# Indirect transfers of a macaron transformer layer, entered by the experts' products instead of at three fixed places of a unit

## The chip, the cores and the metric

The kernel runs on one core of one Trainium2 chip. The metric is device microseconds (us) of one execution. Before the change, three runs took 700.78, 701.87 and 702.69 us; their median is 701.87 us. A separate execution was profiled. TensorE is called PE in the views (its weight loads PEld), VectorE DVE, ScalarE ACT, GpSimd POOL and SyncE SP.

## What is computed

The input x has 8 sequences of 512 tokens with 128 features, in float32. A layer is half a feed-forward step, attention, and another half feed-forward step, each on the layer-normalised x:

```python
x = x + 0.5 * _L0_ffn_ref(_layernorm(x, axis=-1), router_w, router_b, W1, b1, W2, b2)
x = x + _L0_attn_ref(_layernorm(x, axis=-1), w_qkv, w_o, log_xi)
x = x + 0.5 * _L0_ffn_ref(_layernorm(x, axis=-1), router_w, router_b, W1, b1, W2, b2)
```

The feed-forward step is a mixture of 8 experts (128 to 512 to 128 features, ReLU between); a router picks two of them for each token, with a softmax over the two scores as their weights:

```python
logits = jnp.einsum('bsd,de->bse', x, router_w) + router_b
topk_scores, topk_idx = jax.lax.top_k(logits, TOP_K)      # TOP_K = 2
topk_gates = jax.nn.softmax(topk_scores, axis=-1)
...
    h = jax.nn.relu(jnp.einsum('bsd,df->bsf', h_in, w1) + bb1)
    y = jnp.einsum('bsf,fd->bsd', h, w2) + bb2
    return (acc + y * c[..., None], None)                  # c: this expert's weight per token
```

Attention is causal, with 16 heads of 8 features; some heads have a rotary embedding, some a linear decay in the distance.

## The kernel before

**Groups.** Sequences go through the experts in groups: f0 (sequences 0 and 1), f1 (2, 3, 4), f2 (5, 6, 7) for the first feed-forward step, g0, g1, g2 with the same sequences for the last. A group reserves a fixed number of rows for each expert: 351 in f0 and g0, 480 in the others. Four things happen to a group:

- *Routing* (`route`, one call for each sequence) normalises x, takes the router's products, and computes for every token the row of its two experts. The normalisation's reciprocal root, `rstd`, is a `pow` on POOL (recorded at L474, which is the line of the helper `InTurn` through which all such POOL work goes); DVE's four `xn` operations (L769) need it, PE's transposes `xnT_ps` (L784) need those, DVE copies the result (`xnT`, L786), and PE's router products `lg_ps` (L814) follow.
- Eight *scatters* for each sequence (L875) write its tokens to the experts' rows in HBM (`xs`). Each is one indirect DMA that POOL issues, for 128 tokens and one of their two experts.
- The *experts* (`experts`): SP fetches an expert's rows (`xb`, L933); PE transposes them (a `turn`, `xbT_ps`, L976); four *wide* products (`z`, L989) give the hidden features, evicted with ReLU by ACT or DVE (L996, L998); three or four *down* products (`y`, L1013) follow, evicted by DVE (`ysb`, L1017). Turns, wide and down products are the group's *pieces*, which come one at a time from a generator.
- The results come back. For f0, f1, f2 and g0, SP writes an expert's rows to `ys` (L1024), and eight *gathers* for each sequence (`yt`, indirect, L474 through the helper) fetch each token's two rows; DVE adds them to x (L1073). For g1 and g2 every eviction is *sent* to its token's place by an indirect DMA (`ys`, L957), four for each expert, and SP collects whole sequences later (`collect`: `yr`, L1110; DVE adds, L1114; output, L1120).

**Units.** The program is a list of units, numbered -30 to 125, which `surround` (L1427) writes out one after the other. Units 0 to 95 are the *core*: each holds one step of attention (scores, exponentials on ACT, causal mask on DVE, values) with pieces of a group between. Units -30 to -1 (the *prologue*) and 96 to 125 (the *tail*) have no attention; the prologue runs f0's pieces and then f1's, the tail the rest of g1's and all of g2's. `plan` says which group's pieces are run in which units, and each unit takes an equal quota. A table `due` says in which unit the steps of routing, projection, collection and so on come.

**Order.** PE, ACT, DVE and SP run their instructions in the order in which the program was written. POOL's order is fixed by dependencies in `in_turn` (L621): everything that POOL does through the helper comes after all transfers that were entered earlier, and the reverse; only scatters and sends of one run among themselves have no order.

**Transfers.** The indirect transfers wait in two queues of the program's author, not of the chip: `jobs` (scatters and gathers) and `results` (sends). Each call of `transfer` (L650) writes out the next one; with `second=True` it does so only if some job is urgent, or if more than four jobs are queued and no result. `behind_mark` (L635) makes each transfer wait for the eviction of the last wide or down product that was written before it (or for a causal mask in the core); this eviction is its *mark*. In `surround`, `transfer` is called at three fixed places of a unit: after the first piece (L1458), at the end (L1478, `second=True`), and in units from 96 on also at half of the quota when more than two transfers are queued (L1472 to L1475).

Of the kernel before, what the change touches and what calls it, by code (L numbers as in the profile page):

```python
# [21 lines left out]
B, N, D = 8, 512, 128  # L22
# [4 lines left out]
E, FF = 8, 512  # L27
C = FF // P
# [19 lines left out]

ROOMS = [(2, 351, False), (3, 480, False), (3, 480, False), (3, 480, True), (3, 480, True)]
CAP = max(cap for _, cap, _ in ROOMS)  # L50
NOWHERE = 1e6
CT = -(-CAP // P)
STOP = object()
# [395 lines left out]
class Group:  # L449


    def __init__(self, seqs, cap, key, xs, ys, tagged):
        self.seqs, self.cap, self.key, self.xs, self.ys = seqs, cap, key, xs, ys
        self.tagged, self.width = tagged, D + 2 * tagged
        self.ct = -(-cap // P)
        self.rows = cap // self.ct
        assert self.ct * self.rows == cap
        self.parts = [(t, min(3 if cap > 4 * P else 4, self.ct - t))
                      for t in range(0, self.ct, 3 if cap > 4 * P else 4)]
        self.placed = 0  # L460
        self.pieces = E * (len(self.parts) * (1 + C) + self.ct) + 1


# [19 lines left out]
class Main:  # L483
    def __init__(self, tc, ctx, aps):
# [15 lines left out]


        self.jobs, self.results, self.mark = deque(), deque(), None
        self.adds, self.unit = deque(), 0
        const = self.const

# [31 lines left out]
        for e in range(4):  # L537
# [28 lines left out]
            out=before, in_=before, compare_op=ALU.is_gt, fill=0.0, base=0,  # L566
# [8 lines left out]
            out=self.earlier, in_=self.earlier, compare_op=ALU.is_gt, fill=0.0, base=0,  # L575
# [6 lines left out]
            out=self.keep, in_=self.keep, compare_op=ALU.is_ge, fill=0.0, base=0,  # L582
# [67 lines left out]
    def transfer(self, second=False):  # L650

        if self.jobs and (
            not second or any(urgent for urgent, _ in self.jobs)
            or (len(self.jobs) > 4 and not self.results)
        ):
            self.jobs.popleft()[1]()
        elif self.results:
            self.results.popleft()()

    def additions(self):  # L660

# [262 lines left out]
    def experts(self, g):  # L924
# [3 lines left out]
        rows = g.rows  # L928
# [27 lines left out]
        def send(e, t, ys):  # L956
            ins = nc.gpsimd.indirect_dma_start(  # L957
                out=g.ys[:, :],
                out_offset=bass.IndirectOffsetOnAxis(ap=home[e][:rows, t : t + 1], axis=0),
                in_=ys[:rows, t, :], in_offset=None,  # L960
            ).ins
            tc.declare_no_dep(ins, group=f"ys_{key}", reason="no two rows have the same home")
            tc.add_to_no_dep_group(f"ys_{key}", ins)
            self.in_turn(ins, scatter=True)
            self.behind_mark(ins)

        def up(e, xb):

            xT = self.fp.tile([P, CAP], FP, tag="xT", name=f"xT_{key}_{e}")
            h = self.fp.tile([P, C, CAP], FP, tag="h", name=f"h_{key}_{e}")  # L970

            def turn(t0, nt):
                n0, n = t0 * rows, nt * rows
                tp = self.bank([P, N], f"xbT_ps_{key}_{e}_{t0}")
                for t in range(nt):
                    nc.tensor.transpose(  # L976
                        tp[:, ts(t, rows)], xb[:rows, t0 + t, :D], self.ident[:rows, :rows]
                    )
                if self.evac == "act":
                    nc.scalar.copy(xT[:, n0 : n0 + n], tp[:, :n])  # L980
                else:
                    nc.vector.tensor_copy(xT[:, n0 : n0 + n], tp[:, :n])
                if g.tagged and t0 == 0:
                    homes(e, xb)

            def wide(t0, nt, c):
                n0, n = t0 * rows, nt * rows
                z = self.bank([P, N], f"z_{key}_{e}_{n0}_{c}")
                nc.tensor.matmul(  # L989
                    z[:, :n], self.w1_sb[:, e, ts(c, P)], xT[:, n0 : n0 + n],  # L990
                    start=True, stop=True,
                )
                bias = self.b1T[:, e * C + c : e * C + c + 1]
                dst = h[:, c, n0 : n0 + n]
                if self.evac == "act":
                    ins = nc.scalar.activation(dst, z[:, :n], AF.Relu, bias=bias)  # L996
                else:
                    ins = nc.vector.tensor_scalar(dst, z[:, :n], bias, 0.0, ALU.add, ALU.max)  # L998
                self.mark = ins.ins

            return (
                h, [partial(turn, *p) for p in g.parts],
                [partial(wide, *p, c) for p in g.parts for c in range(C)],
            )

        def down(e, h):

            ys = self.fp.tile([P, CT, D], FP, tag="ysb", bufs=5, name=f"ysb_{key}_{e}")

            def out(t):  # L1010
                y = self.bank([P, D], f"y_{key}_{e}_{t}")
                for c in range(C):
                    nc.tensor.matmul(  # L1013
                        y[:rows], h[:, c, ts(t, rows)], self.w2_sb[:, e, c, :],
                        start=(c == 0), stop=(c == C - 1),
                    )
                ins = nc.vector.tensor_tensor(  # L1017
                    ys[:rows, t, :], y[:rows], self.b2_sb[:rows, e], ALU.add
                )
                self.mark = ins.ins  # L1020
                if g.tagged:
                    self.results.append(partial(send, e, t, ys))
                elif t == g.ct - 1:
                    nc.sync.dma_start(  # L1024
                        g.ys[: E * g.cap, :].rearrange("(t p e) d -> e p t d", p=rows, e=E)[e],
                        ys[:rows, : g.ct],
                    )

            return [partial(out, t) for t in range(g.ct)]
# [69 lines left out]
    def collect(self, g, i, dst, parts=1):  # L1099

        nc = self.nc
        b = g.seqs[i]
        x = self.x[b]
        if i % 2 == 0:
            self.pair = self.p2.tile([P, 2, T, 2, D], FP, tag="ee", name=f"yr_{b}")
        yr = self.pair[:, i % 2]
        src = g.ys[2 * N * i : 2 * N * (i + 1), :].rearrange("(t p r) d -> p t r d", p=P, r=2)
        n = T // parts
        for k in range(parts):
            nc.sync.dma_start(yr[:, ts(k, n)], src[:, ts(k, n)])  # L1110
        yield
        for t in range(T):
            for r in range(2):
                nc.vector.scalar_tensor_tensor(  # L1114
                    x[:, t, :], yr[:, t, r], g.gates[:, i, t, r : r + 1], x[:, t, :],
                    ALU.mult, ALU.add,
                )
            if t % n == n - 1:
                k = t // n
                nc.sync.dma_start(  # L1120
                    dst[b].rearrange("(t p) d -> p t d", p=P)[:, ts(k, n)], x[:, ts(k, n)]
                )
            if parts == 1:
                yield
# [179 lines left out]
def macaron_kernel(  # L1304
# [24 lines left out]
    def run(*streams):  # L1329
        for s in streams:  # L1330
            for _ in s:
                pass
# [12 lines left out]
    def take(stream, n):  # L1345

        for _ in range(n):
            if next(stream, STOP) is STOP:
                return
            yield  # L1350
# [5 lines left out]
    with ExitStack() as main:  # L1356
        m = Main(tc, main, aps)
# [8 lines left out]
        g1 = m.open_group([2, 3, 4], 480, 3, "g1")  # L1366
# [33 lines left out]
        def at(u, stream, steps, each=1):  # L1400

            for k in range(steps):
                due.setdefault(u + k // each, []).append((stream, 1))
# [20 lines left out]
        ]  # L1424
        fills = {}

        def surround(n, att):  # L1427

            m.unit = n
# [21 lines left out]
                    m.oT = (*m.held[:2], got)  # L1451
            m.held = (*units[n], ee) if att else None
            m.evac = "dve" if att and n % seq not in (8, 9, 10) else "act"
            run(take(fill, 1 if quota else 0))
            m.evac = "act"
            if att:
                m.causal(units[n][2], ee, 0)
            m.transfer()  # L1458
            if last is not None:
                m.outputs(*last)  # L1460
            if att:
# [5 lines left out]
            for k, (stream, steps) in enumerate(work):  # L1467
                some = todo // (len(work) - k + 1)
                run(take(stream, steps))
                run(take(fill, some))  # L1470
                todo -= some
            if n >= core and len(m.jobs) + len(m.results) > 2:  # L1472
                run(take(fill, todo // 2))
                todo -= todo // 2
                m.transfer(second=True)  # L1475
            run(take(fill, todo))
            m.additions()
            m.transfer(second=True)  # L1478

        m.held = m.oT = None  # L1480
        with m.banks(("m", 8)):
# [34 lines left out]
            for i in range(2):  # L1516
                combined(79 + 7 * i, g0, i, out)
            for i in range(3):
                at(tail + 2 + 3 * i, m.collect(g1, i, out), 5)
            at(tail, m.verdict(bad), 2)  # L1520

            for u in range(first, 0):
# [74 lines left out]
```

## Time and profile before

| | us |
|---|---|
| median of three runs (700.78 to 702.69) | 701.87 |
| the profiled execution | 700.09 |
| span of its trace, first to last instruction | 698.3 |
| PE busy | 629.2 |
| DVE busy / ACT busy / POOL busy | 410.2 / 341.3 / 300.3 |
| first piece of f0 on PE | 40.7 |
| first scores of the core on PE | 142.8 |
| last down product's eviction | 677.8 |
| last send issued / last `yr` adds end | 680.57 / 693.8 |

The trace's clock starts with the first instruction; all times in the text are on it. "Busy" is the time in which an engine has at least one instruction under way. In lists of instructions in order of time, a row has the start, the busy time, engine, line, operation, out<-in, shape and how many were merged; in square brackets stands how long the engine was idle before it and which instruction released it. In tables by stretch of time, each engine has its busy time and, in brackets, its number of instructions; then come the TensorE clock that was granted (1.00 is full speed), the share of the DMA engines' time, and GB/s.

### The profile page before, as it was taken

To read this page: it belongs to the slowest core of one execution; us is meant where nothing else is said; L and a number is where in the kernel's file an instruction comes from. 1 tells how busy PE (TensorE), PEld (TensorE's weight loads), DVE (VectorE), ACT (ScalarE), POOL (GpSimd) and SP (SyncE) were. 2 spreads that over 40 slices of the span, in tenths; PEclk is the share of its full clock that TensorE was granted. 3 is DMA by queue.
4 is the path that set the end of the run, shared out by engine and by line. 5 is a ranking of instruction groups with operands and counts; after the bars stand their busy time and mean duration, and the time that the engine had idled before them with its cause. 6 is when DMAs were issued, how large, how long until landed. Compare 5 with 4: busy or idle time off the path is not lost. (4 is left out here: it accounts for less than half of the span.)

```text
span 698.3 us, 13045 instructions
## 1 busy us (share of the span) xinstructions
PE 629.2 (90%) x4867; PEld 410.3 (59%) x4867; DVE 410.2 (59%) x1442; ACT 341.3 (49%) x548; POOL 300.3 (43%) x322
## 2 busy tenths in 40 slices
PE   3269999999999999999999999999999998969980
PEld 2148867756465656556656656656456656747760
DVE  6736448734466666675687677676666654433414
ACT  4034443455755656565665565555665552234420
POOL 3744637642223223314154423424144556575660
PEclk9999999999999999999999999999999999889995
DMA  8747843312409921111211111101402111145324
GB/s 265 197 136 209 205 115 98 85 45 77 101 22 172 264 69 38 30 29 43 71 32 49 40 38 38 30 27 39 105 27 75 35 31 42 53 121 140 104 58 143
DMA packets 78670, 61.06 MB, mean 87 GB/s; under 512 B 7392, under 2 KB 70792, under 8 KB 78600
## 3 DMA queue, kind: packets, MB, share of 16 engines
q1 hardware_dynamic: 69608, 42.51, 23.8%
q0 software_dynamic: 8704, 17.63, 8.5%
q8 instruction: 41, 0.67, 0.4%
q14 instruction: 29, 0.24, 0.1%
q10 hardware_dynamic: 288, 0.01, 0.0%
HBM read 26.34 MB, written 33.78 MB: 86 GB/s over the span
## 5 line engine op out<-in xcount | busy, mean ns | idle before, releaser
L1208 ACT ACTIVATE ee<-st 128x768 f32<-128x768 f32 (+1 forms) x192 | 159.0, 881 | 104.1 <-PE st L1201 100.6
L474 POOL DMA_INDIRECT yt_f<-ys,back_f x64 | 64.8, 1013 | 133.5 <-DVE ee L1215 55.7
L1215 DVE TENSOR_TENSOR ee<-ee,keep 128x256 f32<-128x256 f32 (+1 forms) x192 | 93.5, 507 | 25.4 <-ACT ee L1208 25.3
L1013 PEld LDWEIGHTS y_g<-w_sb,h_g 128*120 128x120 f32 (+1 forms) x704 | 87.1, 184 | 27.4 <-issue 21.7
L875 POOL DMA_INDIRECT xs<-xn_g,to_g x64 | 63.8, 998 | 90.1 <-DVE ee L1215 34.9
L1013 PEld LDWEIGHTS y_f<-w_sb,h_f 128*120 128x120 f32 (+1 forms) x704 | 85.9, 182 | 28.5 <-issue 16.2
L1201 PE MATMUL st<-qT,kT 32*128 32x512 f32 (+3 forms) x1024 | 96.1, 467 | 2.3 <-ACT h_f L996 0.8
L1013 PE MATMUL y_f<-w_sb,h_f 128*120 128x128 f32 (+1 forms) x704 | 93.9, 277 | 0.2 <-DVE h_f L998 0.2
L989 PE MATMUL z_g<-xT_g,w_sb 128*128 128x480 f32 (+1 forms) x192 | 92.6, 569 | 1.3 <-ACT xT_g L980 1.3
L1013 PE MATMUL y_g<-w_sb,h_g 128*120 128x128 f32 (+1 forms) x704 | 93.0, 277 | 0.6 <-DVE o_tok L1250 0.3
L1227 PE MATMUL o<-ee,vpad 128*32 128x512 f32 (+3 forms) x1024 | 89.4, 442 | 0.8 <-DVE ee L1215 0.8
L989 PE MATMUL z_f<-xT_f,w_sb 128*128 128x480 f32 (+1 forms) x192 | 88.8, 551 | 1.0 <-ACT xT_f L980 1.0
L996 ACT ACTIVATE h_f<-z_f,b1T 128x480 f32<-128x480 f32 (+1 forms) x86 | 53.5, 623 | 68.2 <-PE z_f L989 67.3
L957 POOL DMA_INDIRECT ys<-ysb_g,home_g x64 | 63.7, 996 | 39.3 <-ACT h_g L996 8.7
L1017 DVE TENSOR_TENSOR ysb_f<-y_f,b_sb 120x128 f32<-120x128 f32 (+1 forms) x88 | 25.0, 287 | 77.9 <-PE y_f L1013 74.2
L996 ACT ACTIVATE h_g<-z_g,b1T 128x480 f32<-128x480 f32 (+1 forms) x71 | 45.7, 646 | 47.4 <-PE z_g L989 46.7
L1201 PEld LDWEIGHTS st<-qT,kT 32*128 32x128 f32 x1024 | 43.1, 183 | 32.6 <-issue 8.1
L1017 DVE TENSOR_TENSOR ysb_g<-y_g,b_sb 120x128 f32<-120x128 f32 (+1 forms) x88 | 25.1, 287 | 58.2 <-PE y_g L1013 57.6
L1227 PEld LDWEIGHTS o<-ee,vpad 128*32 128x32 f32 x1024 | 23.5, 108 | 52.4 <-issue 7.5
L875 POOL DMA_INDIRECT xs<-xn_n,to_f x40 | 39.0, 974 | 34.9 <-ACT xi_sb L727 8.1
L989 PEld LDWEIGHTS z_g<-xT_g,w_sb 128*128 128x128 f32 x192 | 30.1, 195 | 26.6 <-issue 15.2
L989 PEld LDWEIGHTS z_f<-xT_f,w_sb 128*128 128x128 f32 x192 | 30.2, 194 | 13.8 <-issue 7.2
(186 smaller groups left out, 778.7 us busy)
## 6 DMA issues: line engine op xcount, KB each, us to landing
w_sb<-in_L_ffn_W_dram SPq DMA_DIRECT2D x16, 256.0 KB
xs<-zeros SPq DMA_DIRECT2D x8, 487.5 KB
xb_g<-xs SPq DMA_DIRECT2D x16, 243.8 KB
xb_f<-xs SPq DMA_DIRECT2D x16, 240.0 KB
ys<-ysb_f SPq DMA_DIRECT2D x16, 240.0 KB
ys<-zeros SPq DMA_DIRECT2D x2, 1536.0 KB
x<-in_L_attn_x_dram SPq DMA_DIRECT2D x8, 256.0 KB
xs<-zeros SPq DMA_DIRECT2D x1, 1920.0 KB
```

What stands on the lines that cost most here:

```text
L474: ins = op(*args, **kw)
L875: ins = nc.gpsimd.indirect_dma_start(out=g.xs[:, :], out_offset=bass.IndirectOffsetOnAxis(ap=g.to[:, i, t, r : r + 1], axis=0), in_=xn[:, ...
L957: ins = nc.gpsimd.indirect_dma_start(out=g.ys[:, :], out_offset=bass.IndirectOffsetOnAxis(ap=home[e][:rows, t : t + 1], axis=0), in_=ys[:r ...
L989: nc.tensor.matmul(z[:, :n], self.w1_sb[:, e, ts(c, P)], xT[:, n0 : n0 + n], start=True, stop=True,)
L996: ins = nc.scalar.activation(dst, z[:, :n], AF.Relu, bias=bias)
L1013: nc.tensor.matmul(y[:rows], h[:, c, ts(t, rows)], self.w2_sb[:, e, c, :], start=(c == 0), stop=(c == C - 1),)
L1017: ins = nc.vector.tensor_tensor(ys[:rows, t, :], y[:rows], self.b2_sb[:rows, e], ALU.add)
L1201: nc.tensor.matmul(st[:, h, c0 : c0 + N - kt * P], kT[r0 : r0 + SLOT, ts(kt, P)], qT[r0 : r0 + SLOT, kt * P :], start=True, stop=True,)
L1208: nc.scalar.activation(ee[:, two, :width], st[:, two, :width], AF.Exp)
L1215: ins = self.nc.vector.tensor_tensor(d, d, self.keep.unsqueeze(1).unsqueeze(1).to_broadcast([P, 2, len(parts), P]), ALU.min,)
L1227: self.nc.tensor.matmul(self.o[h * SLOT : (h + 1) * SLOT, kt * P :], self.vpads[b % 2][:, kt, 4 * g + h, :], ee[:, h, c0 : c0 + n], start= ...
```

## The change

Outside the core, `transfer` is no longer called at fixed places. A counter, `work`, adds up the columns of the experts' products as they are written: the rows of a turn, the rows of a wide product, 512 for a down product, and 350 for each step of other work in a unit outside the core. After any piece outside the core, if `work` is at least 830, `transfer` is called, without the conditions of `second=True`; each call of `transfer` takes 830 off, down to zero. In the core the two calls stay as they were. The collection of g1 starts three units later, and an assertion says that all sends have been written before a collection.

```diff
+SPACING = 830
...
             self.jobs.popleft()[1]()
         elif self.results:
             self.results.popleft()()
+        self.work = max(self.work - SPACING, 0)
...
                     nc.vector.tensor_copy(xT[:, n0 : n0 + n], tp[:, :n])
+                self.work += nt * rows
...
                 self.mark = ins.ins
+                self.work += n
...
                 self.mark = ins.ins
+                self.work += C * D
...
+        def pieces(fill, n, att):
+
+            for _ in take(fill, n):
+                if not att and m.work >= SPACING:
+                    m.transfer()
+                yield
+
...
-            run(take(fill, 1 if quota else 0))
+            run(pieces(fill, 1 if quota else 0, att))
             m.evac = "act"
             if att:
                 m.causal(units[n][2], ee, 0)
-            m.transfer()
+                m.transfer()
...
                 run(take(stream, steps))
-                run(take(fill, some))
+                run(pieces(fill, some, att))
                 todo -= some
-            if n >= core and len(m.jobs) + len(m.results) > 2:
-                run(take(fill, todo // 2))
-                todo -= todo // 2
+                if not att:
+                    m.work += 350
+            run(pieces(fill, todo, att))
+            m.additions()
+            if att:
                 m.transfer(second=True)
-            run(take(fill, todo))
-            m.additions()
-            m.transfer(second=True)
...
-                at(tail + 2 + 3 * i, m.collect(g1, i, out), 5)
+                at(tail + 5 + 3 * i, m.collect(g1, i, out), 5)
```

More of the change, by code (lines that the diff above doesn't have):

```diff
@@ L459, in __init__ @@
                       for t in range(0, self.ct, 3 if cap > 4 * P else 4)]
-        self.placed = 0
+        self.placed = self.sent = 0
         self.pieces = E * (len(self.parts) * (1 + C) + self.ct) + 1
@@ L502, in __init__ @@
         self.jobs, self.results, self.mark = deque(), deque(), None
+        self.work = 0
         self.adds, self.unit = deque(), 0
@@ L965, in send @@
             self.behind_mark(ins)
+            g.sent += 1
         def up(e, xb):
@@ L1106, in collect @@
         yr = self.pair[:, i % 2]
+        assert g.sent == E * g.ct
         src = g.ys[2 * N * i : 2 * N * (i + 1), :].rearrange("(t p r) d -> p t r d", p=P, r=2)
```

## The prediction

> **What bounds the kernel now.** I read the page's slices first, then the chain that ended last, then PE's list of instructions with its gaps, and last the lists of POOL and DVE at those gaps.
>
> ```profile
> PE   3269999999999999999999999999999998969980
> POOL 3744637642223223314154423424144556575660
> PEclk9999999999999999999999999999999999889995
> ```
>
> PE is full from the third slice to the end but for two slices near 590 and 615 us, where the granted clock falls too. POOL is never full in a slice of 17 us. So PE's fixed order sets the time, and POOL matters only where PE waits for it.
>
> ```profile
> 680.57 2.78 DMA ys<-ysb_g,home_g
> 683.37 2.52 DMA yr<-ys
> 685.91 0.36 DVE x L1114
> ```
>
> The chain's end: the last eviction (677.80) is followed by three sends, 1.29 apart, a landing, the collection and its adds. The changed program also has exactly three sends behind the last eviction. This end costs 0 relative to PE's last piece, in both programs.
>
> PE's list has few gaps between 40.7 and 677.5. The rows that I need:
>
> ```profile
> 80.32 1.04 PE L1013 MATMUL y_f<-w_sb,h_f 128*117 128x128 f32 x8
> 81.19 0.60 PE L784 MATMUL xnT_ps_f<-ident,xn_f 128*128 128x128 f32 x4
> ...
> 91.42 0.60 PE L976 MATMUL xbT_ps_f<-ident,xb_f 120*128 120x120 f32 x4 [0.84 <-DMA xb_f<-xs]
> ...
> 589.66 1.26 PE L784 MATMUL xnT_ps_g<-ident,xn_g 128*128 128x128 f32 x4 [1.87 <-DVE xn_g L769]
> 591.71 1.88 PE L814 MATMUL lg_ps_g<-rw_sb,xnT_g 128*128 128x8 f32 x8 [0.78 <-DVE xnT_g L786]
> ...
> 616.69 1.03 PE L976 MATMUL xbT_ps_g<-ident,xb_g 120*128 120x120 f32 x4 [4.67 <-DMA xb_g<-xs]
> ```
>
> In the prologue the transposes of sequence 5 (81.19) come without a gap; in the tail those of sequence 7 (589.66) wait 1.87 for `xn`. POOL and DVE say why:
>
> ```profile
> 76.05 0.96 POOL L875 DMA_INDIRECT xs<-xn_n,to_f  x1 [1.01 <-ACT h_f L996]
> 77.31 0.95 POOL L875 DMA_INDIRECT xs<-xn_n,to_f  x1 [0.30 <-DVE gates_f L912]
> 78.28 1.07 POOL L474 TENSOR_TENSOR rstd_f<-var_f,neg_half 128x4 f32<-128x4 f32 x1
> 79.54 1.04 POOL L875 DMA_INDIRECT xs<-xn_n,to_f  x1 [0.19 <-issue]
> ```
>
> ```profile
> 79.39 1.21 DVE L769 TENSOR_SCALAR xn_f<-x,mv_f,rstd_f 128x128 f32<-128x128 f32 x4 [1.27 <-POOL rstd_f L474]
> ```
>
> The helper's order lets `rstd` (78.28) run only behind the transfers written before it; DVE's four `xn` start 0.04 after `rstd`, PE's last transpose 0.06 after the fourth `xn`. A transfer starts at the later of two times: 1.27 after the one before (0.97 busy, 0.30 idle), or 0.28 after its mark's eviction. In before POOL often stood idle for a mark: 22.8 us ahead of the 24 scatters of f1.
>
> **The change, part by part.** PE's and ACT's orders are unchanged; DVE's moves only in the `x` adds and the collections; the core's program is unchanged but that f2's last scatters are already written. What changes is when transfers are written, so which ones stand ahead of each `rstd`, and their marks. By my walk through both programs, 830 columns are about one to two us of PE work (a down product of 512 columns is four matmuls of 277 ns, a wide one of 480 takes 569 ns), so the queue is emptied about as fast as POOL can go. Four stalls come of it in the prologue.
>
> *S1.* All 16 scatters of sequences 3 and 4 now stand ahead of `rstd` of sequence 5; the first waits for the eviction that ends at 61.13. First 61.40, last 61.40+15x1.27 = 80.45, ended 81.41. `rstd` 81.42 to 82.49 (before 78.28 to 79.35), `xn` from 82.53, fourth transpose 82.53+1.21+0.06 = 83.80, where it was 81.52: PE waits +2.28. Behind it, the fetch of f1's first expert: its scatters now end about 10 us earlier, but SP's write of expert 6's rows is queued ahead of it (eviction 87.41), so it starts at 87.41+2.28+0.36 = 90.05 instead of 88.38, +1.67. PE takes up the rest in its 0.84 and 0.57 of gaps at 91.42 and 92.68: lateness falls to 1.69.
>
> *S2.* Eight gathers of sequence 0 and two scatters of sequence 5 now stand ahead of `rstd` of sequence 6 (before: six gathers). First mark 94.45+1.69, first start 96.42, tenth 107.85, ended 108.83; `rstd` to 109.89; last transpose 109.93+1.11+0.06 = 111.10 against 107.67+1.69 = 109.36: +1.74, in all 3.43.
>
> *S3.* Ten more (six scatters, four gathers of sequence 1) stand ahead of `rstd` of sequence 7: 110.08 to 122.48; two `rstd` (this one and the attention's first) end at 123.53 and 124.53, where they ended at 118.36. Transposes 124.74 against 119.1+3.43 = 122.53: +2.21, in all 5.64.
>
> *S4.* Two gathers of sequence 1 come behind those `rstd`, at 124.72 and 125.99, landed at 128.49 (2.5, as other gathers). DVE's adds wait for them and stand ahead of the `xnT` copies; the router products start at 129.95 instead of 122.85+5.64 = 128.49: +1.46, in all 7.10. Of this 0.45 goes in the wait for `qpad` (0.88 at 136.81), since the projections ahead of it are not all late. The core begins about +6.6 late.
>
> *Tail.* One gather less stands ahead of `rstd` of sequence 7 (it starts at 586.80, was 588.16): the 1.87 gap shrinks by 1.35. One pair of DVE adds moves ahead of the `xnT` copy: +0.65. Scatters of that sequence remain bound by POOL, back to back before and after; the 4.67 gap stays. g1's sends end about 5 us later, and its collections come three units later with them; DVE's wait for them (5.58 at 639.06) cost PE nothing and is covered. Were that cover gone, the collection would be late by at most the same 5 us, with some 40 us left to the end. Net -0.7.
>
> Sum of stalls +6.6-0.7 = +5.9.
>
> *The clock.* The trace has no prologue stretch at half clock; its neighbours in kind are these (from:to, length, PE busy, PEld, DVE, ACT, POOL, granted clock, DMA share, GB/s):
>
> ```profile
> 86.07:92.89 6.82, 5.42 (x45) 4.64 (x44) 3.63 (x15) 1.67 (x3) 0.96 (x1) 1.00 0.53 146
> ...
> 584.41:591.24 6.83, 4.55 (x25) 2.88 (x23) 3.34 (x17) 1.32 (x2) 5.46 (x6) 1.00 0.12 35
> 591.24:598.06 6.82, 6.35 (x28) 5.35 (x29) 3.44 (x13) 1.22 (x2) 3.57 (x4) 0.50 0.10 29
> ```
>
> PE idle 2.28 in one stretch was followed by a stretch granted 0.50; idle 1.40 was not. A half-clock stretch costs half of the PE work in it, 6.35/2 = 3.2, less where PE waits anyway (2.7). S1 (2.28) reaches the row that fell, S3 (2.21) comes just under it, S2 (1.74) lies nearer to 1.40 and S4 (1.46) at it. Between the ends 0 and 4x3 I take one stretch, S1's: +2.7. In the tail 0.5+0.78+0.65 and a residue of small gaps still come near 2.3 in one stretch, so I leave the half clock after 591; were it gone, -3.2.
>
> The Trainium skill, in "TensorE: Matmul & The Clock Gate", section "HAM oscillation — how this bites in real kernels", warns only of idle gaps above about 3.4 us. By that rule none of my stalls would lower the clock and the sum would be 5.9 alone; but here the clock fell after 584.41:591.24, whose largest single gap was 1.87, so I let the measured rows decide.
>
> Total on the profiled execution: 700.09 (its span is 698.3) +5.9+2.7 = 708.7. The median of the runs lies 1.78 above that execution, so 710.5; I say 710.
>
> **The rivals.**
>
> *R2, the stalls come but the clock holds.* For: the stretches lie on a fixed grid of 6.83 us, and an idle of 2.28 can fall across two. Against: the tail's fell at just that sum. 701.87+5.9 = 707.8.
>
> *R3, the clock falls two or three times.* For: S3 is 0.07 below the row that fell, and prologue gaps of 0.1 add to each. 710+3 to 710+6: 713 to 716.
>
> *R1, faster.* One mechanism: `rstd` of sequence 7 in the tail comes a transfer earlier, PE's idle in that stretch falls below the row that tripped the clock, and the half clock after 591 goes: -1.35+0.65-3.2 = -3.9; with prologue stalls covered, 698. For: the tail's slack is tight at 2.28 and the edit cuts into it. Against: it needs the prologue's stalls to total less than 3.9, where rows give 6.6; that decides. It holds if scatters start earlier than their marks let me think, or if POOL's 1.27 falls to its busy 0.97: 16 scatters then end 4.5 earlier, and S1 is gone.
>
> *R4, the change does not do what it says.* POOL's 1.27 a transfer sets the pace wherever many are queued, so another spacing only reorders them, and transfers ahead of `rstd` replace those that in before came ahead of the next one. For: POOL is back to back from 600.92 to 636.77 already. Against: the 22.8 us of idle in the prologue. 702.
>
> **How the numbers follow.** 0.3% is 2.1 us, about what a measurement can tell from no change. Main (stalls and one half-clock stretch) 0.40, 710; R2 0.22, 707.8; R3 0.18, 713 to 716; R1 0.13, 698; R4 0.07, 702. Slower 0.40+0.22+0.18 = 0.80, faster 0.13, same 0.07. The least of the slower cases has S4 gone, 0.88 taken up at `qpad` and no half clock: 1.69+1.74+2.21-0.88-0.7 = +4.1, 705.9; with the tail's half clock gone too, 702.7. The most is R3's 716. The range 703 to 716 leaves out R1 and R4, 2 in 10.
>
> **What would show it.** Right: POOL's list has `rstd_f` at about 82, 109 and 123 us, each directly behind a run of transfers at 1.27; DVE's `xn_f` has idle time put to `rstd_f`; PE's list has gaps ahead of `xnT_ps_f` of about 2.3, 1.7 and 2.2, and one of 1.5 ahead of `lg_ps_f`; a stretch of the prologue shows a clock of 0.50; the core's first scores come at 149 to 152 instead of 142.8; the gap at 589.66 is near 0.5; the end has three sends behind the last eviction. S1 is wrong if `rstd_f` starts before 80; the clock's term if no stretch before 150 shows under 1.00. The whole is wrong if the core's first scores come before 146, or if PE's gaps in the tail change by more than 3 us.

## The result and the profile after

The changed kernel takes 705.87 us (median of 7 executions, 703.85 to 708.62), the one before 701.87 (7 executions): a ratio of 1.0063, 95% interval 1.0042 to 1.0083. So it is 2.9 to 5.8 us slower. The profiled execution took 708.19 us with a span of 706.4; it is one of the three longest of the seven, and this matters below.

The slices of the changed kernel, in tenths of full:

```profile
PE   3269999899999999999999999999999998979980
POOL 3755527750041314414144513415144546657760
PEclk9999999999999999999999999999999999889995
```

POOL now works early and then stands still: its tenth and eleventh slices, 159 to 194 us, are zero, where the page of before has 2 and 2. PE has a new dent in its eighth slice, 124 to 141 us. The list of PE's instructions, those with idle time ahead of them in the prologue and in the tail:

```profile
83.90 1.00 PE L787 MATMUL xnT_ps_f<-ident,xn_f 128*128 128x128 f32 x4 [1.61 <-DVE xn_f L772]
113.56 1.25 PE L787 MATMUL xnT_ps_f<-ident,xn_f 128*128 128x128 f32 x4 [1.33 <-DVE xn_f L772]
127.58 1.10 PE L787 MATMUL xnT_ps_f<-ident,xn_f 128*128 128x128 f32 x4 [2.04 <-DVE xn_f L772]
...
598.08 1.09 PE L787 MATMUL xnT_ps_g<-ident,xn_g 128*128 128x128 f32 x4 [0.53 <-DVE xn_g L772]
600.49 1.87 PE L817 MATMUL lg_ps_g<-rw_sb,xnT_g 128*128 128x8 f32 x8 [1.31 <-DVE xnT_g L789]
...
624.41 1.03 PE L980 MATMUL xbT_ps_g<-ident,xb_g 120*128 120x120 f32 x4 [3.48 <-DMA xb_g<-xs]
```

Three waits for `xn` are new, one for each of sequences 5, 6 and 7. In the tail the wait for `xn` is down from 1.87 to 0.53, the one for `xnT` up from 0.78 to 1.31, and the one for the fetch down from 4.67 to 3.48. POOL's list says what is ahead of the three `rstd`:

```profile
81.33 0.96 POOL L878 DMA_INDIRECT xs<-xn_n,to_f  x1 [0.31 <-issue]
82.31 1.06 POOL L475 TENSOR_TENSOR rstd_f<-var_f,neg_half 128x4 f32<-128x4 f32 x1
...
111.07 0.99 POOL L878 DMA_INDIRECT xs<-xn_f,to_f  x1 [0.30 <-issue]
112.07 1.05 POOL L475 TENSOR_TENSOR rstd_f<-var_f,neg_half 128x4 f32<-128x4 f32 x1
...
125.10 0.95 POOL L475 DMA_INDIRECT yt_f<-ys,back_f  x1 [0.30 <-issue]
126.06 1.08 POOL L475 TENSOR_TENSOR rstd_f<-var_f,neg_half 128x4 f32<-128x4 f32 x1
```

Each `rstd` follows the last of a run of transfers with no pause. DVE's list has the `xn` that wait for them, and ahead of the second an add that waits for a gather (one stands ahead of the third too, at 125.05 after 1.36 us of idle time):

```profile
83.41 1.11 DVE L772 TENSOR_SCALAR xn_f<-x,mv_f,rstd_f 128x128 f32<-128x128 f32 x4 [4.44 <-POOL rstd_f L475]
...
112.28 0.35 DVE L1080 SCALAR_TENSOR_TENSOR x<-yt_f,gates_f,x 128x128 f32<-128x128 f32 x1 [0.89 <-DMA yt_f<-ys,back_f]
113.16 1.27 DVE L772 TENSOR_SCALAR xn_f<-x,mv_f,rstd_f 128x128 f32<-128x128 f32 x4 [0.53 <-POOL rstd_f L475]
...
127.18 1.12 DVE L772 TENSOR_SCALAR xn_f<-x,mv_f,rstd_f 128x128 f32<-128x128 f32 x4 [0.18 <-POOL rstd_f L475]
```

And the clock, from the table by stretch (PE, PEld, DVE, ACT, POOL busy, then the granted clock):

```profile
81.46:84.87 3.41, 1.80 (x13) 1.35 (x12) 1.46 (x6) 0.55 (x1) 1.89 (x2) 1.00 0.73 194
84.87:88.29 3.42, 3.42 (x13) 2.66 (x12) 1.03 (x3) 0.55 (x1) 0.00 (x0) 0.50 0.22 63
...
122.42:129.25 6.83, 4.75 (x28) 2.85 (x27) 5.04 (x29) 1.57 (x3) 5.87 (x6) 1.00 0.34 96
129.25:132.66 3.41, 3.41 (x12) 2.66 (x13) 1.65 (x7) 0.00 (x0) 2.50 (x4) 0.50 0.15 38
```

Two stretches of the prologue fell to half clock (a granted clock of 0.50), each 3.41 us long and each after a stretch in which PE was idle for 1.6 to 2.1 us. The end is as it was: in the chain that ended last the send starts at 688.99, the collected rows are there at 694.03, and the adds run to 701.94.

Since PE's order is the same in both kernels, every one of its 4867 matmuls can be set against the same one of before. The table holds how much later it starts in the changed kernel and in three experiments (told below; all lateness in us against the profiled execution of before, each step being the difference of two such numbers).

| step (its time in before) | forecast | changed | tail_fixed | fill_pro | rstd_early |
|---|---|---|---|---|---|
| clock's first rise to full (up to 60) | none | +0.94 | +0.73 | +0.18 | +1.57 |
| S1, sequence 5 (82.2) | +2.28 | +2.6 | +2.17 | +2.18 | 0.00 |
| half clock after it (83.7) | +2.7, once | +1.2 | none | none | none |
| fetch of f1's first expert (91.4) | -0.59 | -0.06 | -0.21 | -0.17 | -0.12 |
| S2, sequence 6 (108.2) | +1.74 | +2.14 | +2.17 | +2.15 | +1.49 |
| S3, sequence 7 (119.8) | +2.21 | +2.24 | +2.30 | +2.26 | +2.10 |
| half clock after it (122.5) | none | +1.7 | none | none | none |
| S4, `lg_ps_f` (124.1) | +1.46 | 0.0 | +1.7 | +1.8 | +1.1 |
| wait for `qpad` (137.7) | -0.45 | -1.1 | -1.1 | -1.0 | -1.1 |
| first scores of the core (142.8) | +6.6 | +9.78 | +7.79 | +7.43 | +5.18 |
| tail, to the last product | -0.7 | -1.5 | +0.1 | -1.2 | -3.0 |

In S1 of the changed kernel 0.4 belongs to the half-clock stretch that begins in it.

### The profile page after: what moved, and what is told of

The parts are those of the page before. It is cut to its first block, busy times and chain, and to the rows that moved or that the text cites. A ratio compares the mean times of both kernels' runs of the same rounds, so it can differ in the third digit from the quotient of the medians.

```text
span 706.4 us, 13046 instructions
## 1 busy us (share of the span) xinstructions
PE 635.9 (90%) x4867; PEld 413.8 (59%) x4867; DVE 410.7 (58%) x1442; ACT 341.1 (48%) x548; POOL 300.6 (43%) x322
## 5 line engine op out<-in xcount | busy, mean ns | idle before, releaser
L1019 PEld LDWEIGHTS y_f<-w_sb,h_f 128*120 128x120 f32 (+1 forms) x704 | 87.9, 186 | 29.3 <-issue 17.3
L1019 PE MATMUL y_f<-w_sb,h_f 128*120 128x128 f32 (+1 forms) x704 | 95.7, 280 | 0.2 <-DVE h_f L1003 0.2
L994 PE MATMUL z_f<-xT_f,w_sb 128*128 128x480 f32 (+1 forms) x192 | 91.6, 567 | 1.0 <-ACT xT_f L984 1.0
L878 POOL DMA_INDIRECT xs<-xn_n,to_f x40 | 38.9, 972 | 30.6 <-ACT h_f L1001 12.9
```

The source lines that it names most:

```text
L878: ins = nc.gpsimd.indirect_dma_start(out=g.xs[:, :], out_offset=bass.IndirectOffsetOnAxis(ap=g.to[:, i, t, r : r + 1], axis=0), in_=xn[:, ...
L994: nc.tensor.matmul(z[:, :n], self.w1_sb[:, e, ts(c, P)], xT[:, n0 : n0 + n], start=True, stop=True,)
L1019: nc.tensor.matmul(y[:rows], h[:, c, ts(t, rows)], self.w2_sb[:, e, c, :], start=(c == 0), stop=(c == C - 1),)
```

## The experiments

### One part alone

`pro_fixed` puts the fixed places back for the prologue and keeps the tail; `tail_fixed` the reverse, with the earlier collection. The first:

```diff
-                if not att and m.work >= SPACING:
+                if not att and m.unit >= 0 and m.work >= SPACING:
...
-            if att:
+            if att or n < 0:
                 m.transfer()
...
-            if att:
+            if att or n < 0:
                 m.transfer(second=True)
```

The second, cut to its core:

```diff
-                if not att and m.work >= SPACING:
+                if n < 0 and m.work >= SPACING:
...
+            if n >= core and len(m.jobs) + len(m.results) > 2:
+                run(take(fill, todo // 2))
+                todo -= todo // 2
+                m.transfer()
...
-                at(tail + 5 + 3 * i, m.collect(g1, i, out), 5)
+                at(tail + 2 + 3 * i, m.collect(g1, i, out), 5)
```

> Kernel: the changed one, with the fixed places again in the prologue; the tail and the later collection as changed. Theory (POOL's backlog ahead of rstd in the prologue costs the time, the tail gains): first scores of the core at about 143 us as in before, no gap ahead of xnT_ps_f, tail gaps as in the changed kernel (7.4 us, before 9.4), so about 701.9 - 2.0 = 699.9 us, 699 to 701. Rival (the loss sits in the tail, in the later collection): 704 us or more, with the core starting early all the same.

> Kernel: the changed one, with the fixed places and the earlier collection again in the tail; the prologue as changed. Theory: the three waits ahead of xnT_ps_f stay (1.3 to 2.1 us each), the core starts at 149 to 153 us, the tail gap ahead of xnT_ps_g is 1.9 us again and the one ahead of xbT_ps_g 4.7, so about 705.9 + 2.0 = 707.9 us, 706.5 to 709.5. Rival (the loss sits in the tail): 703 us or less.

Measured, beside a kernel before at 701.38 us (17 executions): `pro_fixed` 698.46 us, ratio 0.9961 (0.9949 to 0.9974); `tail_fixed` 707.29, ratio 1.0085 (1.0071 to 1.0099). So the prologue costs 5.9 us and the tail gains 2.9. Their sum, +3.0, lies just within the interval of the whole change, 2.9 to 5.8. The rival is out in both runs, but `pro_fixed` came out under the 699 to 701 us that were expected: the tail gained more than its gaps. `pro_fixed` is faster than both kernels of the case.

In PE's list of `tail_fixed` the three waits stand as in the changed kernel (1.60, 1.36 and 2.10), and there is a fourth, which the changed kernel's profile does not have:

```profile
83.68 1.01 PE L787 MATMUL xnT_ps_f<-ident,xn_f 128*128 128x128 f32 x4 [1.60 <-DVE xn_f L772]
...
131.60 1.06 PE L817 MATMUL lg_ps_f<-rw_sb,xnT_f 128*128 128x8 f32 x8 [1.28 <-DVE xnT_f L789]
```

This is S4. It shows here because no stretch of this execution's prologue ran at half clock. In the changed kernel's profile PE was slowed by 1.7 us just ahead of that place, so the copy was there when PE came: by this reading the half clock and S4 share one price. The times agree with it. Three of the five executions of `tail_fixed` have a mean clock of 0.975, about one stretch of 3.41 us at half clock more than the 0.978 of the profiled one, and took no longer for it (706.75 to 707.29 against 707.60 and 708.53 us); where that stretch lies, no profile shows.

Table by stretch of `pro_fixed`, in the tail:

```profile
586.83:593.66 6.83, 4.99 (x32) 3.67 (x31) 3.68 (x17) 1.14 (x3) 4.33 (x5) 1.00 0.24 66
593.66:597.07 3.41, 3.41 (x16) 2.62 (x15) 2.88 (x13) 1.06 (x2) 2.80 (x3) 0.50 0.20 54
```

PE is idle 1.84 us here, 2.28 in before, and the half clock lasts 3.41 us instead of 6.83. That, 3.41/2 = 1.7 less, is the larger part of what the tail gained beyond the forecast (-3.0 instead of -0.7).

### `rstd` ahead of the transfers

Every transfer and its place stay as in the changed kernel; only statistics, `var` and `rstd` of sequences 5, 6 and 7 are written earlier.

```diff
+EARLY = (-25, -17, -14)
...
+            for b, u in ((5, EARLY[0]), (6, EARLY[1]), (7, EARLY[2])):
+                if n == u:
+                    m.begun[b] = m.layernorm(m.x[b], f"f2_{b}")
+                if n in (u, u + 1):
+                    next(m.begun[b])
...
+        elif b in self.begun:
+            yield
+            yield
+            xn = yield from self.begun.pop(b)
```

> Kernel: the changed one, in which statistics, var and rstd of sequences 5, 6 and 7 are written three or four units earlier, so that POOL has them ahead of the transfers; every transfer stays. Theory (PE waits for rstd alone): no gap ahead of xnT_ps_f of sequences 5 and 6 and about 4 us less lateness; rstd_a of the attention's first sequence still stands behind 12 transfers (about 123 us by POOL's steps of 1.27), so the third wait stays, now ahead of xnT_ps_a, at 2 to 4 us; time 702 to 704 us. Rival (the transfers themselves slow PE, DVE or the fetches by contention, whatever the order of rstd): gaps and time as in the changed kernel, 705 to 708 us.

Measured: 702.35 us (11 executions, 700.64 to 705.03), ratio 1.0018 (1.0005 to 1.0031). The time is as expected and the rival is out: with the same transfers, most of the loss is gone. S1 vanished whole (table). But a wait for sequence 6 stayed, which was not expected, and the one for sequence 7 stands ahead of `xnT_ps_f`, not of `xnT_ps_a`. PE's list, and then DVE's just ahead of the two waits:

```profile
109.85 1.03 PE L788 MATMUL xnT_ps_f<-ident,xn_f 128*128 128x128 f32 x4 [0.90 <-DVE xn_f L773]
123.52 1.09 PE L788 MATMUL xnT_ps_f<-ident,xn_f 128*128 128x128 f32 x4 [1.79 <-DVE xn_f L773]
```

```profile
109.11 0.35 DVE L1085 SCALAR_TENSOR_TENSOR x<-yt_f,gates_f,x 128x128 f32<-128x128 f32 x1 [1.03 <-DMA yt_f<-ys,back_f]
...
120.88 0.35 DVE L1085 SCALAR_TENSOR_TENSOR x<-yt_f,gates_f,x 128x128 f32<-128x128 f32 x1 [1.61 <-DMA yt_f<-ys,back_f]
```

DVE waits not for `rstd` but for a gather. The adds come two units after the gather is written, and with POOL behind, a gather written early lands late; DVE's order then holds `xn` back behind the add. So the backlog reaches PE by two ways, `rstd` and the adds, that in the changed kernel end almost together (the add of sequence 6 at 112.63, its `rstd` at 113.12). The prediction saw the second way only at S4.

### PE kept busy in the waits

```diff
+        if self.unit < 0 and key in ('f2_5', 'f2_6', 'f2_7'):
+            for t in range(16):
+                nc.tensor.transpose(tp[:, ts(t % T, P)], self.ident, self.ident)
         for t in range(T):
             nc.tensor.transpose(tp[:, ts(t, P)], xn[:, t, :D], self.ident)
```

> Kernel: the changed one, with 16 more transposes of the identity (about 0.11 us each, 1.75 us) ahead of the transposes of sequences 5, 6 and 7, into the same bank, so that PE is busy while it waits. Theory (the clock falls for PE's idle time): the ends of the three waits stay where they are, no stretch of the prologue has a clock of 0.50, every run has a mean clock of about 0.98, and the time is that of the best runs of the changed kernel, 703.5 to 705 us. Rival (the clock falls for another reason): half-clock stretches in the prologue stay, some runs still take 707 to 709 us. If the work does not fit into the waits, up to 2 us more.

Measured: 705.65 us (6 executions, 704.55 to 707.09), ratio 1.0059 (1.0045 to 1.0073). No stretch of the prologue is at half clock in the profile, and no execution has a mean clock under 0.978, where the changed kernel has 0.973, 0.976 and 0.976 beside four of 0.980. That is as expected, and the spread halved (2.5 us, 4.8 in the changed kernel). It does not show that idle time alone sets the clock: the profiled execution of `tail_fixed`, without the added work, has waits of 1.60, 1.36 and 2.10 us at the same places and keeps the full clock there too. Nor did the median come into the expected 703.5 to 705. The three executions with a mean clock of 0.980 took 704.55 to 705.35 us; the three with 0.978 took 705.95 to 707.09, and the profiled one of these has two half-clock stretches of 6.83 us in the tail. S4 appears in full (a wait of 1.38 ahead of `lg_ps_f`) where in the changed kernel's profile the half clock had hidden it.

### Three series in which the kernel before takes 716 us

The next eight runs fell on other chips, on which the kernel before itself took 716.7, 716.2 and 715.8 us. The changed kernel was not run there. The kernels: `rstd_adds_hold` is `rstd_early` with later adds and with no transfers in four units; `adds_late` is the changed kernel with later adds; `pro_fixed_fill` and `before_fill` have transposes of the identity in the waits of the tail. Of the cuts below, the first is in `adds_late` and `rstd_adds_hold`, the second in `rstd_adds_hold` alone, and the third is one of three such places in `pro_fixed_fill`.

```diff
-                self.adds.append((self.unit + 2, partial(add, t, [yts[t, 0], yts[t, 1]])))
+                late = (3 if b == 0 else 4) if self.unit < 0 else 2
+                self.adds.append((self.unit + late, partial(add, t, [yts[t, 0], yts[t, 1]])))
...
-                if not att and m.work >= SPACING:
+                if not att and m.work >= SPACING and not -12 <= m.unit <= -9:
...
+        if key == 'g2_7':
+            for t in range(10):
+                nc.tensor.transpose(lp[:, ts(t % T, P)], self.ident, self.ident)
```

> Kernel: that with the early rstd of sequences 5, 6 and 7; besides, DVE's adds of gathered rows are written one unit (sequence 0) or two units (sequence 1) later in the prologue, and no transfer is written in units -12 to -9, so that rstd_a comes ahead of eight more transfers. The spacing of 830 stays. Theory (PE waits for rstd behind POOL's backlog and for DVE's adds behind late gathers, and for nothing else): no gap ahead of xnT_ps_f, xnT_ps_a or lg_ps_f, first scores of the core at 143 to 145 us, time 698 to 700 us, as with the fixed places in the prologue (698.5). Rival (transfers close together slow the fetches or PE by themselves): 701.5 us or more, with the lateness at other places.

> Kernel: the changed one, with DVE's adds of gathered rows written one unit (sequence 0) or two units (sequence 1) later in the prologue, nothing else. Theory (S4 is the adds that wait for gathers issued behind rstd): the gap ahead of lg_ps_f (1.3 us in runs without a slow stretch at that place) is gone, the three ahead of xnT_ps_f stay; 704.0 to 705.0 us against 705.9. Rival (these adds do not hold up anything, or rstd's wait only grows into their place): 705.5 to 706.5 us.

> Kernel: that with the fixed places in the prologue and the changed tail; besides, transposes of the identity into banks that are overwritten afterwards, 4, 10 and 28 of them, where PE waits in the tail (0.53, 1.31 and 3.39 us). Theory (the clock falls after a stretch with 1.6 us or more of idle PE): no stretch at 0.50 before the last eviction, mean clock 0.985 or more, and 1.7 us (a stretch of 3.41) and 2.9 us (one of 6.83) less, 694 us, 693 to 695.5. Rival (the clock does not follow PE's idle time): 698 to 699 us and the same two slow stretches.

> Kernel: the one before, with 15, 6 and 38 transposes of the identity at the three waits of the tail (1.87, 0.78 and 4.67 us). Theory (clock by idle PE): no stretch at 0.50 before the last eviction, 3.2 and 2.3 us less (half of the PE work in the two stretches), 696 us, 695 to 697.5. Rival (clock by another cause): 701 to 702 us.

Measured, as ratios to the kernel before on the same chip: `rstd_adds_hold` 1.0168 (1.0140 to 1.0196), `adds_late` 1.0321 (1.0295 to 1.0346), `pro_fixed_fill` 0.9990 (0.9973 to 1.0006), `before_fill` 1.0009 (0.9983 to 1.0034). All four miss what was expected: the core's first scores of `rstd_adds_hold` come at 165.15 us instead of 143 to 145, those of `adds_late` at 172.59. Three of the kernels ran again:

> The same kernel as in the series in which the kernel before itself took 716.7 us and its engines waited for nothing that the profile shows; again, to have it beside a kernel before at about 701.5. Theory as then: no gap ahead of xnT_ps_f, xnT_ps_a or lg_ps_f, no wait for issue, first scores of the core at 143 to 145 us, 698 to 700 us. Rival (transfers close together slow the fetches, the instruction supply or PE by themselves): 701.5 us or more, with the lateness at other places, as the 12.5 us more than before in that series would have it.

> The same kernel again, for the same reason. Theory as then: the gap ahead of lg_ps_f is gone, the three ahead of xnT_ps_f stay; 704.0 to 705.0 us where the changed kernel takes 705.9. Rival (rstd's wait grows into the place of the adds, or they hold up nothing): 705.5 to 706.5 us.

> The same kernel again, for the same reason. Theory (the clock follows PE's idle time): no stretch at 0.50 between the first product and the last eviction, mean clock 0.985 or more, 693 to 695.5 us. Rival (it does not): 698 to 699 us and the same two slow stretches. Third: the added transposes are supplied too slowly and run beyond the waits: over 699 us.

> The same kernel a third time. If the kernel before takes about 701.5 us beside it: theory (rstd behind the backlog and adds behind late gathers are all that PE waits for in the prologue): no gap ahead of xnT_ps_f, xnT_ps_a or lg_ps_f, first scores of the core at 143 to 146 us, 698 to 700 us; rival (dense transfers slow the instruction supply or PE): 701.5 us or more and waits for issue. If before takes about 716 us: 729 us again, and the cause of the waits for issue stays open.

Measured: `rstd_adds_hold_2` 1.0180 (1.0150 to 1.0210), `adds_late_2` 1.0286 (1.0255 to 1.0316), `pro_fixed_fill_2` 0.9977 (0.9951 to 1.0003), `rstd_adds_hold_3` 1.0156 (1.0125 to 1.0188). PE's list of `adds_late_2` and, below it, of `rstd_adds_hold_3`:

```profile
85.48 0.78 PE L1019 MATMUL y_f<-w_sb,h_f 128*117 128x128 f32 x2 [4.87 <-issue]
...
121.40 1.10 PE L787 MATMUL xnT_ps_f<-ident,xn_f 128*128 128x128 f32 x4 [1.09 <-DVE xn_f L772]
135.13 0.21 PE L847 MATMUL pos_ps_f<-mask_f,earlier 128*128 128x32 bf16 x1 [4.60 <-DVE mask_f L840]
```

```profile
81.87 0.70 PE L1024 MATMUL y_f<-w_sb,h_f 128*117 128x128 f32 x2 [2.11 <-issue]
...
88.77 1.01 PE L788 MATMUL xnT_ps_f<-ident,xn_f 128*128 128x128 f32 x4 [0.38 <-ACT h_f L1006]
...
161.04 2.09 PE L1215 MATMUL st<-qT,kT 32*128 32x512 f32 x8 [7.82 <-DVE ysb_f L1028]
```

On these chips PE, ACT, DVE and POOL wait in places where the profile shows no releaser ("issue", "remote"). Waits of this kind of over 0.4 us, from 45 us to the core's first scores, summed over the four engines by the lists of each run:

| kernel | prologue's transfers | us |
|---|---|---|
| before, changed, `pro_fixed`, `tail_fixed`, `fill_pro` (the first series and the prediction's pair) | both | 0 |
| `rstd_early` (the first series) | spaced | 0.7 |
| `before_fill` / `pro_fixed_fill` (two runs) | fixed places | 7.8 / 8.3, 11.4 |
| `rstd_adds_hold` (three runs) | spaced, with a pause | 22.0, 30.6, 12.2 |
| `adds_late` (two runs) | spaced | 23.8, 33.3 |

What follows is limited. The places agree with the theory in part: in the three runs of `rstd_adds_hold` no wait ahead of `xnT_ps_f` or `lg_ps_f` is left that `xn`, `rstd` or a gather ends, and neither run of `adds_late` has one ahead of `lg_ps_f`. But of the three waits ahead of `xnT_ps_f` that should have stayed, `adds_late` has two and `adds_late_2` one. The times do not test the theory, because other waits take the place of those that went. In `rstd_adds_hold` PE waits 7.82 to 8.76 us ahead of the core's first scores for an eviction (`ysb_f`), and shortly before it DVE stood idle for 4.2 to 5.0 us without a releaser. On one chip the kernels with spaced transfers in the prologue have 2.7 to 3.1 times the sum of those with fixed places (on the third chip there is nothing to compare with), and in `adds_late` PE stands still for "issue" at 81 to 83 us, among the last of 16 scatters, the last ten of which follow each other without a pause. That speaks for the rival of these runs, a price of dense transfers as such, which the first chip does not show. It does not show it: all spaced kernels on these chips have the later adds as well, and the changed kernel, which has not, was not run there. What the engines wait for was not found and stays open.

The filler in the tail says more about the clock than about the time. In all six profiles without it (before, changed, `pro_fixed`, `tail_fixed`, `rstd_early`, `fill_pro`) a half-clock stretch follows the waits at `xnT_ps_g` and `lg_ps_g`; in the three with it, where these waits are 0.23 us or less, none does. The half-clock stretches that remain in the tail stand behind idle time that the filler left or that came anew: 1.92 and 2.35 us in `pro_fixed_fill_2`, and up to 1.77 for "issue" inside the filler itself in `before_fill`. That agrees with the theory that idle PE brings the half clock on, though no amount of it was found that always does, and no profile of these kernels without filler was taken on the same chips. What full filler would save stays open.

## Why the prediction was right, and where it was not

*Bound and mechanism.* Right. PE's fixed order sets the time, the core did not move (lateness 9.78 at its first scores, 9.75 near its end), the end costs nothing (span and last product differ by 8.1 and 8.3), and the loss is POOL's backlog, ahead of `rstd` and ahead of the gathers. `rstd_f` was forecast at 81.42 and came at 82.31, behind 16 scatters at steps of 1.25 to 1.33, the first of them 0.94 later than forecast, as PE itself was by then. The other two came at 112.07 and 126.06, where 109 and 123 were forecast, since PE was 3 us later than forecast behind the fetch (4.73 instead of 1.69).

*Two readings.* The spacing is shorter than the prediction says: PE's matmuls overlap, and in its list of before the eight that begin at 52.08, two down products or 1024 columns, are followed by the next at 52.95. So 830 columns of products are 0.70 us and not "about one to two us", which makes the backlog surer. And of the 22.8 us that POOL "stood idle for a mark", 8.1 lie ahead of the first scatter, and up to 0.30 for each of the others is the step between transfers; by POOL's list about 8 us are left that could be used.

*S1 to S4.* Right in place and nearly in size. Without a half clock, S1 to S4 measured 2.17, 2.17, 2.30 and 1.7 (`tail_fixed`) against 2.28, 1.74, 2.21 and 1.46. S2 is larger since its ten transfers took up to 1.38 a step and the `xn` 1.27, not 1.11. The fetch gave back 0.2 and not 0.59; the wait for `qpad` 1.1 and not 0.45. The sum to the core, 7.1 without the clock's first rise (7.79 - 0.73), stands against 6.6.

*The clock in the prologue.* The step "I take one stretch, S1's: +2.7" is mis-sized. A stretch in the prologue lasted 3.41 us, not 6.83; in the changed kernel's profile there were two, worth 1.2 and 1.7, and the second only took the place of S4. The "fixed grid of 6.83 us" does not fit before's own trace either: its half-clock stretches begin at 591.24 and 615.13, 3.5 times 6.83 apart and 7 times 3.41. Most executions probably had none in the prologue. A mean clock of 0.980 at 704 us means some 28 us at half clock (2 x 0.020 x 704), of which 17.4 lie between the last product and the end of the trace; what is left, about 10.8, has room for three stretches of 3.41 and not for four. In the profiles of `pro_fixed` and `rstd_early`, 0.980 as well, all three lie in the tail; of the four such executions of the changed kernel no profile was kept. So R2, stalls without the clock, is the likelier account of these four, and the main case that of the profiled one, whose 708.19 us the forecast of 708.7 met by luck, with errors that cancelled: the prologue came to 9.8 (0.9 of it the clock's first rise) instead of 6.6 + 2.7, the tail to -1.5 instead of -0.7.

*The tail.* The step "Scatters of that sequence remain bound by POOL, back to back before and after; the 4.67 gap stays" is wrong. In POOL's list of before two scatters and a pause of 1.40 stand ahead of the last six; in the changed kernel three and a pause of 0.69 ahead of the last five:

```profile
602.22 0.98 POOL L875 DMA_INDIRECT xs<-xn_g,to_g  x1 [0.30 <-issue]
604.60 0.97 POOL L875 DMA_INDIRECT xs<-xn_g,to_g  x1 [1.40 <-issue]
```

```profile
611.94 0.97 POOL L878 DMA_INDIRECT xs<-xn_g,to_g  x1 [0.30 <-ACT h_g L1001]
613.60 0.97 POOL L878 DMA_INDIRECT xs<-xn_g,to_g  x1 [0.69 <-issue]
```

One more scatter of 1.27 went out ahead of the pause, whose releaser the profile does not show, and PE's wait for the fetch behind them is 1.19 shorter. The other two terms hold: -1.34 against -1.35 at `xn`, +0.53 against +0.65 at `xnT`. A fourth, +0.66, is in no forecast: PE comes back earlier in the half-clock stretch behind the fetch, so 5.96 us of its work fall into it instead of 4.62. And "so I leave the half clock after 591" holds in the profiled execution and in that of `fill_pro`; in those of `pro_fixed` and `rstd_early` it is halved. The tail is then worth -3.0 and not -0.7. R1 had this mechanism with -3.9; its other half, a covered prologue, did not come.

*The median.* With the prologue at 7.1 (`tail_fixed`) and the tail at -3.0 (`pro_fixed`, `rstd_early`) the sum is +4.1; the medians differ by 4.0. That they agree so closely is luck: the two halves' medians add up to +3.0. The forecast of 710 was too high by the prologue's half clock, 2.7, and by the tail's gain, 2.3 more than forecast, and too low by 0.5 in the stalls. The first is a term of the clock, the second for the larger part.

*The rule on gaps.* In the changed kernel's profile idle time of 1.61 us in a stretch of 3.41, in one gap, was followed by half clock; in `tail_fixed`'s a gap of 1.60 was not. The Trainium skill's rule in "TensorE: Matmul & The Clock Gate", section "HAM oscillation — how this bites in real kernels", names gaps of about 3.4 us. Here the measurement decides: much shorter gaps were enough in some executions. The median of 705.87 us still came nearer to the rule's result, 5.9 of stalls alone (707.8), than to the main case of 710.

## What to carry to other kernels

A queue that is emptied as fast as its engine can go is a queue in front of everything else on that engine: before spacing work more densely, list the short instructions that others wait for (here a `pow` of 1.06 us) and count what will stand ahead of each. Consumers that are placed a fixed distance after a transfer is *written*, such as the adds here, have to be moved as well when the issue falls behind the writing. And a change that has a good and a bad half is worth running by halves: the tail's spacing with the old prologue is 0.4% faster than the kernel before, in the one series in which it ran.

## What was not expected of the hardware

- The time at which the clock first became full varied from 45.10 to 48.07 us among the six profiled executions of before, the changed kernel and the first four experiments, though PE began at 40.4 to 40.9; a rise 2.4 us later than in before (47.53) left PE of `pro_fixed` 1.07 us later.
- Half-clock stretches lasted 3.41 or 6.83 us; waits of PE of 1.61 and 2.04 us in the prologue were followed by one in the changed kernel's profile, waits of 1.60 and 2.10 at the same places in `tail_fixed`'s by none. The mean clock of the changed kernel's executions went from 0.973 to 0.980.
- One program, the kernel before, took 701 us on one chip and 712 to 722 on three others; the kernels profiled there have waits on several engines for which the profile shows no releaser.
